# A two-layer graph transformer on one core: where the attention steps stand in the feed-forward loop, and the order of a block's last matmuls

## The chip, the cores and the metric

The kernel runs on one core of a Trainium2 chip. The metric is the device time of one execution in microseconds; the median of three runs is compared.

## The reference

There are 2708 nodes with 512 features each, and an adjacency matrix that is symmetric, sparse and has ones on the diagonal. Two layers of the same form, with weights of their own, follow each other. All is float32.

```python
mask = adj + eye(n)
q, k, v = (h @ W.T + b).reshape(n, 8, 64)            # for Wq, Wk, Wv
scores = einsum('nhd,mhd->hnm', q, k) / sqrt(64)
scores = where(mask == 0, -1e9, scores)
ctx = einsum('hnm,mhd->nhd', softmax(scores), v).reshape(n, 512)
h1 = layer_norm(h + ctx @ Wo.T + bo)
h2 = layer_norm(h1 + relu(h1 @ W1.T + b1) @ W2.T + b2)   # W1: 2048 x 512, W2: 512 x 2048
```

## The kernel before

The first stage turns the adjacency matrix into lists of neighbours. The nodes are sorted by the length of their lists and cut into 22 tiles of up to 128 nodes, so that all the nodes of a tile need about equally many neighbours: from 22 (tile 0) down to 3 (tile 21). The attention of a tile gathers its neighbours' keys and values row by row with indirect DMAs that POOL issues (`gather`, L976), in steps of two neighbours.

Tiles are worked on in pairs, called blocks. Tile 21, the last, has only 20 nodes. There are 11 blocks to a layer, in this order: (21, 20), (19, 18), (8, 9), (7, 10), (6, 11), (0, 17), (1, 16), (2, 15), (3, 14), (4, 13), (5, 12). I number them k = 0 to 10.

The feed-forward part of a block (`feed_forward`) runs over 16 chunks f of 128 hidden units. For each chunk TensorE makes `pf` (the first matrix product, L1290), ScalarE turns it into `ft` with a relu (L1298), and TensorE adds the second product into the accumulators `a0` and `a1` of the block's two tiles (`second`, L1278). The second product runs LAG = 3 chunks behind the first. The last three chunks of it therefore come after the loop, in what I call the tail of the block. `pf` has three buffers in PSUM, `ft` four in SBUF.

The attention of later blocks is written between those chunks. `attend` is a generator, and each turn of it issues one step: VectorE multiplies the gathered keys with the queries (`kv`, L1013) and sums them to scores (`sc`, L1019); one turn later ScalarE takes two exponentials (`p`, L1032) and scales the values by them with eight instructions (`kv` or `acc`, L1039), and VectorE scales the other half (L1045) and adds (L1052). After a tile's last step ScalarE divides with eight instructions (L1083), and the tile's context `cx` is ready. There are three `cx` buffers.

How many turns are taken is set by `advance`. Each call adds credit, at most 1.5 in all; turns are taken while there is credit and fewer than CXB - 1 = 2 contexts wait in `got`. The main loop calls it after each chunk, with PACE (0.62 in the first layer, 0.72 in the second), or with 1.1 or 0.4 in block 0.

In chunk 10 of a block (11 in the very first) `through(k + 1)` takes whatever turns are still missing for the contexts of the next block. Then `attended` turns the two contexts around (TensorE `tp`, L1122; ScalarE `cT`, L1127), and in the next chunk it multiplies them with Wo (`o`, L569) and normalizes the sum (`h`). After chunk 15 `turned` turns `h` around on TensorE, and ScalarE writes it as `hT` in eight copies (L1127). `hT` is the input of the next block's first `pf`. At the beginning of a block VectorE adds `a0` and `a1` to `h` (L1310) and normalizes; in the first layer `keys_values` then makes keys and values for the second layer in chunks 5 to 8.

TensorE, ScalarE and SyncE run in the order in which the program is written. VectorE and POOL run in an order that the framework chooses, except in some stages ahead of the blocks and, for POOL, in block 0 of the first layer. [...]

Of the kernel before, what the change touches and what calls it, by code (L numbers as in the profile page):

```python
# [25 lines left out]
NFC = FF // P  # L26
# [12 lines left out]
LAG = 3  # L39
KVB = 5  # L40
CXB = 3
# [7 lines left out]
PACE = (0.62, 0.72)  # L49
# [422 lines left out]
def by_edges(ctx: ExitStack, tc: tile.TileContext, x, xT, adj, layers, out, good):  # L472
# [57 lines left out]
    def matrix(w, name, tag, by=None):  # L530
        src = chunked(w[name])
        t = wts.tile([P, src.shape[1], src.shape[2]], F32, tag=tag, name=tag)
        if by:
            by.dma_start(out=t, in_=src)
            return t
        k = max(1, src.shape[1] // 4)
        for c in range(0, src.shape[1], k):
            nc.sync.dma_start(out=t[:, c : c + k, :], in_=src[:, c : c + k, :])
        return t
# [32 lines left out]
    def finish(steps):  # L572
        for _ in steps:
            pass
# [6 lines left out]
    def size(g):  # L581
        return min(P, N - g * P)
# [520 lines left out]
    def norm(z, r, gain, shift):  # L1103

        st = small.tile([P, 6], F32, tag="st", name="st")
        nc.vector.bn_stats(st[:r], z[:r])  # L1106
        mv = small.tile([P, 2], F32, tag="mv", name="mv")
        nc.vector.bn_aggr(mv[:r], st[:r])
        va = small.tile([P, 1], F32, tag="va", name="va")
        nc.vector.tensor_scalar(va[:r], mv[:r, 1:2], EPS, None, ALU.add)  # L1110
        rd = small.tile([P, 1], F32, tag="rd", name="rd")
        nc.gpsimd.tensor_tensor(rd[:r], va[:r], mhalf[:r], ALU.pow)  # L1112
        nc.vector.scalar_tensor_tensor(
            z[:r], z[:r], mv[:r, 0:1], gain[:r], ALU.subtract, ALU.mult
        )
        nc.vector.scalar_tensor_tensor(z[:r], z[:r], rd[:r], shift[:r], ALU.mult, ALU.add)  # L1116
# [14 lines left out]
    class Layer:  # L1131
# [133 lines left out]
        def feed_forward(self, block, hs, hT):  # L1265

            w = sum(size(g) for g in block)
            accs = [ps_a.tile([P, DM], F32, tag=f"a{i}", name=f"a{i}") for i in range(len(block))]
            fts = []

            def second(f, only=None):
                c0 = 0
                for g, a in zip(block, accs):
                    r = size(g)
                    if only not in (None, g):
                        c0 += r
                        continue
                    nc.tensor.matmul(  # L1278
                        a[:r],
                        fts[f][:, c0 : c0 + r],  # L1280
                        self.w2[f // 2][:, f % 2, :],
                        start=(f == 0),
                        stop=(f == NFC - 1),
                    )
                    c0 += r

            for f in range(NFC):
                pf = ps_f.tile([P, DM], F32, tag="f", name="pf")
                for c in range(NC):
                    nc.tensor.matmul(  # L1290
                        pf[:, :w],
                        self.w1[f // 2][:, c, f % 2 * P : f % 2 * P + P],
                        hT[:, c, :w],
                        start=(c == 0),
                        stop=(c == NC - 1),
                    )
                ft = dn.tile([P, 2 * P], F32, tag="ft", name="ft", bufs=4)
                nc.scalar.activation(ft[:, :w], pf[:, :w], AF.Relu, bias=self.b1[:, f : f + 1])  # L1298
                fts.append(ft)
                if f >= LAG:  # L1300
                    second(f - LAG)
                yield None
            for g in block:
                for f in range(NFC - LAG, NFC):
                    second(f, g)
            zs = []
            for g, a, h in zip(block, accs, hs):
                r = size(g)
                z = h
                nc.vector.tensor_tensor(z[:r], a[:r], h[:r], ALU.add)  # L1310
                norm(z, r, self.g2, self.e2)
                if self.n == NL - 1:
                    nc.gpsimd.indirect_dma_start(  # L1313
                        out=out,
                        out_offset=bass.IndirectOffsetOnAxis(ap=ident_i[:r, g : g + 1], axis=0),
                        in_=z[:r],
                        in_offset=None,
                        bounds_check=N - 1,
                        oob_is_err=False,
                    )  # L1320
                zs.append(z)
            yield zs
# [41 lines left out]
    blocks = [(NT - 1, NT - 2), (NT - 3, NT - 4)] + [  # L1364
        (i, NT - 5 - i) for i in (*range(8, 5, -1), *range(6))
    ]
    NB = len(blocks)
    order = [g for block in blocks for g in block]
# [47 lines left out]
    credit = 0.0  # L1416

    def advance(more):

        nonlocal credit  # L1420
        credit = min(credit + more, 1.5)
        while credit > 0 and len(got) < CXB - 1:
            cost = next(ahead, None)
            if cost is None:
                break
            credit -= cost

    def through(k):

        while blocks[k][-1] not in got:  # L1430
            next(ahead)

    got = {}
# [38 lines left out]
    for n in range(NL):  # L1472
        last = n == NL - 1
        nxt = None if last else Layer(n + 1, layers[n + 1])
        if n > 0:
            streamed = now.queries(order[8 : 2 * AHEAD])
            got = {}
# [25 lines left out]
        for k, block in enumerate(blocks):  # L1503
            more = k + 1 < NB
            asking = iter(())
            if n > 0 and k + AHEAD < NB:
                asking = now.queries(blocks[k + AHEAD])
            for f, zs in enumerate(now.feed_forward(block, hs, hT)):
                if f == NFC:
                    break  # L1510
                if f in (5, 6, 7, 8) and behind:
                    next(behind)
                if more and f == 10 + (k + n == 0):
                    through(k + 1)
                    projecting = now.attended(blocks[k + 1], got)
                    next(projecting)
                if more and f == 11 + (k + n == 0):
                    for hs_next in projecting:
                        advance(0.5 if k else 0.0)
                advance(PACE[n] if k else 1.1 if f < 11 else 0.4)  # L1520
                if f in (0, 3, 7, 9):
                    next(asking, None)
                if more and f == NFC - 1:
                    finish(asking)
                    hT = now.turned(blocks[k + 1], hs_next)
                if k == 0 and len(now.w1) < NFC // 2 and f % 2 == 0:
                    now.load_w1(len(now.w1), nc.scalar)
                    now.load_w2(len(now.w2), nc.scalar)
                if n > 0 and (k, f) == (0, 2):
                    now.load_second(1, temp)  # L1530
                if not last:
                    if (k, f) == (0, 10):
                        now.load_next()
                        now.kv = [matrix(nxt.w, "Wk", "wk", nc.scalar)]
                    if (k, f) == (0, 13):
                        now.kv.append(matrix(nxt.w, "Wv", "wv", nc.scalar))
                    if (k, f) == (3, 2):
                        now.wq = matrix(nxt.w, "Wq", "wq")
                    if f == 1 and k in (1, 3):
                        i, name, scale = (1, "bk", 1.0) if k == 1 else (0, "bq", DK**-0.5)  # L1540
                        turning = turned_row(now.cols[i], name, scale)
                        rows_of = now if k == 1 else nxt
                        setattr(rows_of, name, next(turning))
                    if f == 3 and k in (1, 3):
                        finish(turning)
                if not last and not more:
                    if f % 2:
                        nxt.load_w1(f // 2)
                        if f > 2:
                            nxt.load_w2(f // 2 - 1)  # L1550
                    if f == 6:
                        nxt.load_first()
                        nxt.load_second(0, temp)
                    if f == 7:
                        finish(ahead)
                        pool += nxt.preloaded(order[:8], temp)
            in_order.close()
            if not last:
                behind = now.keys_values(block, zs)
            if more:  # L1560
                hs = hs_next
# [76 lines left out]
```

## Time and profile before

| what | value |
|---|---|
| median of three runs | 1969.64 us (1968.0 to 1970.87) |
| the profiled execution | 1975.51 us, its span 1973.8 us |
| TensorE busy | 1902.7 us, 96% of the span |
| VectorE busy | 1300.5 us, 66% |
| ScalarE busy | 933.5 us, 47% |
| POOL busy | 794.1 us, 40% |
| mean granted TensorE clock | 0.985 |

The profiled execution took 1.7 us more than its span, and 5.9 us more than the median of the runs. The span has these parts: keys, values and the neighbour lists of the first layer (to 170 us), its queries (to 275 us), its 11 blocks (to 1141 us), a stage of queries again (to 1238 us), and the second layer's blocks. [...] Lost time is better seen where a matmul starts later than the one before it allows. The share of VectorE in the whole span says little, because the last two blocks of each layer have next to no attention left, while others are full of it.

### The profile page before, as it was taken

What the parts mean: (1) busy time and instruction counts of PE and PEld (TensorE: products, weight loads), DVE (VectorE), ACT (ScalarE), POOL (GpSimd) and SP (SyncE); (2) the same over time, 40 slices, a digit from 0 to 9 for tenths busy, and PEclk for the clock granted to TensorE, in tenths of its full rate; (3) what the DMA queues carried; (4) which work ended last, traced back from release to release, by engine and by line L of the source; (5) the groups of instructions that cost most, each with busy time, mean ns of one, the idle gap of its engine ahead of it and who ended that gap; (6) DMA issues with size and microseconds to landing.
All of it is one profiled execution on the core that took longest, in us unless ns stands there. A gap on an engine that the chain in (4) does not pass through costs nothing. (4 is left out here: it accounts for less than half of the span.)

```text
span 1973.8 us, 20851 instructions
## 1 busy us (share of the span) xinstructions
PE 1902.7 (96%) x6150; PEld 1102.7 (56%) x6150; DVE 1300.5 (66%) x2141; ACT 933.5 (47%) x3218; POOL 794.1 (40%) x710
## 2 busy tenths in 40 slices
PE   8999989999999999999999998999999999999997
PEld 4443344565656556566566643556666566666664
DVE  6884577684957869558442026887688988877421
ACT  4560244464555655547442112756456765755310
POOL 3114435453645636435210022555346655544210
PEclk9999999999999999999999999999999999999998
DMA  9998667454645647445310646856455766554100
GB/s 331 348 307 286 216 223 258 160 174 166 223 149 190 215 158 237 156 161 187 132 58 22 224 155 231 284 182 215 153 184 192 250 201 221 181 192 148 39 11 13
DMA packets 131487, 366.92 MB, mean 186 GB/s; under 512 B 16669, under 2 KB 36989, under 8 KB 128655
## 3 DMA queue, kind: packets, MB, share of 16 engines
q0 software_dynamic: 69120, 246.35, 37.8%
q1 hardware_dynamic: 53332, 99.66, 14.8%
q10 hardware_dynamic: 8910, 19.48, 2.6%
q8 instruction: 50, 0.82, 0.2%
q14 instruction: 75, 0.61, 0.1%
HBM read 314.62 MB, written 50.83 MB: 185 GB/s over the span
## 5 line engine op out<-in xcount | busy, mean ns | idle before, releaser
L976 POOL DMA_INDIRECT kv<-kv_d,idx x420 | 545.0, 1298 | 475.7 <-DVE acc L1052 313.5
L1278 PE MATMUL a<-w,ft 128*128 128x512 f32 (+1 forms) x1408 | 665.8, 598 | 11.0 <-ACT ft L1298 9.4
L1290 PE MATMUL pf<-hT,w 128*128 128x256 f32 (+1 forms) x2816 | 639.9, 374 | 14.4 <-ACT ft L1298 9.9
L1290 PEld LDWEIGHTS pf<-hT,w 128*128 128x128 f32 x2816 | 523.4, 192 | 193.5 <-issue 106.9
L1278 PEld LDWEIGHTS a<-w,ft 128*128 128x128 f32 (+1 forms) x1408 | 255.8, 186 | 236.6 <-issue 198.7
L1298 ACT ACTIVATE ft<-pf,b 128x256 f32<-128x256 f32 (+1 forms) x352 | 158.5, 459 | 434.0 <-PE pf L1290 433.6
L1013 DVE TENSOR_TENSOR kv<-kv,q 128x1024 f32<-128x1024 f32 (+3 forms) x222 | 256.4, 1158 | 155.0 <-DMA kv<-kv_d,idx 90.3
L1039 ACT ACTIVATE kv<-kv,p 128x64 f32<-128x64 f32 x1232 | 311.0, 334 | 5.0
L1019 DVE TENSOR_REDUCE sc<-kv 128x16 f32<-128x1024 f32 (+3 forms) x222 | 255.0, 1154 | 1.4
L1052 DVE TENSOR_TENSOR acc<-acc,kv 128x1024 f32<-128x1024 f32 (+2 forms) x178 | 203.9, 1146 | 28.7 <-ACT kv L1039 27.9
L1112 POOL TENSOR_TENSOR rd<-va,mhalf 128x1 f32<-128x1 f32 (+1 forms) x88 | 85.2, 968 | 272.2 <-DVE va L1110 270.5
L1032 ACT ACTIVATE p<-sc,minus 128x8 f32<-128x8 f32 (+1 forms) x420 | 103.3, 295 | 154.3 <-DVE sc L1019 154.0
L1045 DVE TENSOR_TENSOR kv<-kv,p 128x512 f32<-128x512 f32 (+1 forms) x178 | 121.5, 683 | 55.8 <-ACT p L1032 55.8
L569 PE MATMUL o<-wo,cT 128*128 128x512 f32 (+1 forms) x352 | 155.1, 593 | 0.5 <-ACT cT L1127 0.5
L569 PEld LDWEIGHTS o<-wo,cT 128*128 128x128 f32 (+1 forms) x352 | 65.1, 186 | 86.5 <-issue 74.5
L1083 ACT ACTIVATE cx<-acc,su 128x64 f32<-128x64 f32 (+1 forms) x352 | 88.4, 333 | 37.8 <-DVE su L1075 31.3
L1310 DVE TENSOR_TENSOR h<-a,h 128x512 f32<-128x512 f32 (+1 forms) x44 | 29.7, 677 | 106.8 <-PE a L1278 106.7
L1116 DVE SCALAR_TENSOR_TENSOR h<-h,rd,ln_b 128x512 f32<-128x512 f32 (+1 forms) x88 | 65.8, 748 | 50.8 <-POOL rd L1112 50.8
L663 ACT ACTIVATE code<-aj 128x2708 bf16<-128x2708 int32 (+1 forms) x22 | 73.3, 3333 | 48.7 <-POOL aj L659 47.4
L666 DVE MAX8 tops<-code 128x8 f32<-128x247 f32 (+2 forms) x242 | 83.1, 400 | 19.2 <-ACT code L663 19.2
L1349 POOL DMA_INDIRECT kv_d<-kvs,ident_i x22 | 23.7, 1078 | 178.7 <-ACT kvs L1343 112.6
L1039 ACT ACTIVATE acc<-kv,p 128x64 f32<-128x64 f32 (+1 forms) x352 | 88.8, 334 | 1.4
(133 smaller groups left out, 1517.0 us busy)
## 6 DMA issues: line engine op xcount, KB each, us to landing
aj<-in_adj SPq DMA_DIRECT2D x21, 1354.0 KB, 7.6
kv_d<-kvs ACTq DMA_DIRECT2D x21, 512.0 KB, 7.0
w<-in_W SPq DMA_DIRECT2D x20, 512.0 KB, 4.7
xg<-in_xT SPq DMA_DIRECT2D x19, 512.0 KB, 8.2
kv<-kv_d,idx POOLq DMA_INDIRECT x420, 5.6
w<-in_W ACTq DMA_DIRECT2D x12, 512.0 KB, 6.0
q_d<-qs SPq DMA_DIRECT2D x22, 256.0 KB, 3.1
zT_d<-zT SPq DMA_DIRECT2D x22, 256.0 KB, 4.8
```

The source lines that it names most:

```text
L569: nc.tensor.matmul(o[:r], xs(c), wm[:, c, :], start=(c == 0), stop=(c == NC - 1))
L976: nc.gpsimd.indirect_dma_start(out=to, out_offset=None, in_=table[:, :], in_offset=bass.IndirectOffsetOnAxis(ap=s, axis=0), bounds_check=N ...
L1013: nc.vector.tensor_tensor(kv[:r, :c, :DM], kv[:r, :c, :DM], self.q[:r].unsqueeze(1).to_broadcast([r, c, DM]), ALU.mult,)
L1019: nc.vector.tensor_reduce(self.sc[:r, s0 : s0 + c, :], kv[:r, :c, :DM].rearrange("p s (h d) -> p s h d", d=DK), AX.X, ALU.add,)
L1032: nc.scalar.activation(p[:r, s, :], self.sc[:r, s, :], AF.Exp, bias=minus[:r, g, s : s + 1])
L1039: nc.scalar.activation(to[:, i, hd], kv[:r, i, DM + h * DK : DM + (h + 1) * DK], AF.Copy, scale=p[:r, s0 + i, h : h + 1],)
L1045: nc.vector.tensor_tensor(to[:, 0, :].rearrange("p (h d) -> p h d", d=DK), kv[:r, 0, DM:].rearrange("p (h d) -> p h d", d=DK), p[:r, s0, : ...
L1052: nc.vector.tensor_tensor(self.acc[:r, :c, :], self.acc[:r, :c, :], kv[:r, :c, DM:], ALU.add)
L1083: nc.scalar.activation(cx[:r, hd], self.acc[:r, 0, hd], AF.Copy, scale=self.su[:r, h : h + 1])
L1278: nc.tensor.matmul(a[:r], fts[f][:, c0 : c0 + r], self.w2[f // 2][:, f % 2, :], start=(f == 0), stop=(f == NFC - 1),)
L1290: nc.tensor.matmul(pf[:, :w], self.w1[f // 2][:, c, f % 2 * P : f % 2 * P + P], hT[:, c, :w], start=(c == 0), stop=(c == NC - 1),)
L1298: nc.scalar.activation(ft[:, :w], pf[:, :w], AF.Relu, bias=self.b1[:, f : f + 1])
```

## The change

Three edits.

1. In the tail of a block, the last three chunks of the second product are issued chunk by chunk, each for both tiles: 13 for the block's first and second tile, then 14 for both, then 15 for both. Before, all three came for the first tile and then all three for the second. The last block of a layer keeps the old order.
2. A third context may wait in `got`. With two waiting, turns go on only where the newer of the two has an odd place of at least 5 in the order of tiles (counted from 0), which means that it is the second tile of its block, from block 2 on.
3. In block 0 of the first layer no attention is issued after chunk 1.

```diff
@@ feed_forward
-            for g in block:
+            if block == blocks[-1]:
+                for g in block:
+                    for f in range(NFC - LAG, NFC):
+                        second(f, g)
+            else:
                 for f in range(NFC - LAG, NFC):
-                    second(f, g)
+                    second(f)
@@ advance
         credit = min(credit + more, 1.5)
-        while credit > 0 and len(got) < CXB - 1:
+        while credit > 0 and len(got) < CXB:
+            newest = max(map(order.index, got), default=0)
+            if len(got) == CXB - 1 and (newest < 5 or newest % 2 == 0):
+                break
             cost = next(ahead, None)
@@ main loop
-                advance(PACE[n] if k else 1.1 if f < 11 else 0.4)
+                if n or k or f != 1:
+                    advance(PACE[n] if k else 1.1 if f < 11 else 0.4)
```

## The prediction

> **What bounds the kernel now.** I read the page's busy times first, then a table of stretches, one for each block (from a block's first `pf` to the next block's), and then the instructions in order of time around the gaps.
>
> ```profile
> span 1973.8 us, 20851 instructions
> PE 1902.7 (96%) x6150; PEld 1102.7 (56%) x6150; DVE 1300.5 (66%) x2141; ACT 933.5 (47%) x3218; POOL 794.1 (40%) x710
> ```
>
> TensorE is the bound: every block waits for it in the end. The table's columns are the stretch, its length, then PE, PEld, DVE, ACT and POOL busy. The first three lines are blocks 3, 4 and 9 of layer one, the others blocks 2, 3, 4, 5 and 9 of layer two.
>
> ```profile
> 513.06:592.27 79.21, 79.21 (x273) 48.97 (x272) 55.30 (x75) 40.74 (x152) 38.79 (x31) 1.00 0.54 178
> 592.27:679.59 87.32, 81.88 (x266) 49.43 (x264) 69.31 (x91) 49.42 (x189) 50.16 (x38) 0.96 0.62 202
> 999.92:1078.24 78.32, 78.32 (x266) 48.08 (x265) 22.04 (x45) 19.93 (x63) 7.26 (x7) 1.00 0.07 27
> 1372.15:1444.77 72.62, 71.01 (x241) 43.91 (x239) 50.60 (x76) 36.23 (x137) 32.17 (x27) 1.00 0.55 178
> 1444.77:1508.99 64.22, 63.98 (x224) 41.09 (x224) 50.01 (x66) 35.04 (x132) 33.50 (x25) 1.00 0.50 172
> 1508.99:1578.77 69.78, 66.64 (x225) 42.50 (x226) 67.86 (x93) 47.28 (x182) 46.27 (x35) 0.98 0.74 244
> 1578.77:1647.24 68.47, 65.67 (x225) 41.66 (x224) 60.04 (x83) 43.72 (x168) 37.60 (x32) 0.98 0.66 220
> 1841.36:1905.18 63.82, 63.82 (x225) 41.28 (x225) 17.33 (x44) 14.53 (x44) 6.32 (x7) 1.00 0.02 9
> ```
>
> Blocks 9 have no attention beside them, so 78.3 and 63.8 us are the price of TensorE's work alone (block 3's 79.2 has a turned row more). What a block takes above that is all that a better order can win. By the same table layer one's blocks 1, 2, 4, 5, 6, 7 and 8 exceed it by 3.0, 8.2, 9.0, 2.7, 2.6, 0.9 and 0.9 us; layer two's 2 to 8 by 2.0, 0.4, 6.0, 4.7, 0.4, 0.4 and 2.0 (block 2 against block 1, which also projects queries). Together 43 us, and block 0 of layer one comes on top:
>
> ```profile
> 287.50 2.34 PE L1290 MATMUL pf<-hT,w 128*128 128x148 f32 x8 [5.97 <-ACT ft L1298]
> ...
> 304.17 2.12 PE L1290 MATMUL pf<-hT,w 128*128 128x148 f32 x8 [2.70 <-ACT ft L1298]
> ...
> 308.94 1.17 PE L1290 MATMUL pf<-hT,w 128*128 128x148 f32 x8
> ```
>
> Two waits for `ft`, and behind each a `pf` that takes 2.1 to 2.3 us in place of 1.17. ScalarE at that time:
>
> ```profile
> 284.64 0.49 ACT L1032 ACTIVATE p<-sc,minus 128x8 f32<-128x8 f32 x2 [5.29 <-DVE sc L1019]
> ...
> 287.09 0.36 ACT L1298 ACTIVATE ft<-pf,b 128x148 f32<-128x148 f32 x1
> ...
> 289.79 2.00 ACT L1083 ACTIVATE cx<-acc,su 128x64 f32<-128x64 f32 x8
> 291.70 0.36 ACT L1298 ACTIVATE ft<-pf,b 128x148 f32<-128x148 f32 x1
> ```
>
> An exponential waits for VectorE, and `ft` 1 stands behind it. Then ScalarE has no pause until 300 us. The largest later wait is at block 4's turning of the contexts:
>
> ```profile
> 643.95 1.91 PE L1122 MATMUL tp<-ident,cx 128*128 128x128 f32 x4 [3.75 <-ACT cx L1083]
> 645.65 3.62 PE L1290 MATMUL pf<-hT,w 128*128 128x256 f32 x8
> ...
> 657.71 1.89 PE L1290 MATMUL pf<-hT,w 128*128 128x256 f32 x8
> ```
>
> And a tail with attention after chunk 15, the end of block 5:
>
> ```profile
> 757.31 2.02 ACT L1083 ACTIVATE cx<-acc,su 128x64 f32<-128x64 f32 x8
> 759.23 2.14 ACT L1127 ACTIVATE hT<-tp,b 128x128 f32<-128x128 f32 x8
> 760.64 2.66 PE L1290 MATMUL pf<-hT,w 128*128 128x256 f32 x8 [2.27 <-ACT hT L1127]
> ```
>
> [...] block 4 of layer two is busy for 66.6 of 69.8 us and still 6.0 us over. [...] here waits of 2.27 us and more are followed by `pf` at up to twice its time[...], and each avoided long wait saves up to 1.7 us more. [...]
>
> **The change, part by part.** Numbers of instructions stay the same; only places change.
>
> *No attention after chunk 1.* One step and one division move from ahead of `ft` 2 to behind it: 2 exponentials (0.48), 8 scalings (2.0) and 8 divisions (2.0), 4.5 us. `ft` 1 keeps its place, so the 5.97 us stay. `ft` 2 comes at 287.8, `ft` 3 to 5 at 292.6, 295.7 and 298.4, each ahead of TensorE's chunk. Late next is `ft` 6 at 304.1, wanted at 304.3. The second wait goes (2.70), and the slow matmuls behind it (0.95 for `pf`, 0.8 for `a`). **Gain 4.4 us**, between 0 and 4.5. VectorE has the same steps one chunk later, with chunks 6 to 10 free of attention behind them. ScalarE's own weight loads for chunk 10 on keep their order and are issued within 1 us of their present times; I cost them at nothing.
>
> *The tail by chunks.* The first tile's product of chunk 14 is wanted 0.86 us later and that of 15 1.72 us later (a product takes 0.86). But the next block's first `pf` needs five of the eight `hT` copies, which ScalarE takes up only after `ft` 15 and the step behind it. In most tails with a wait they set the end as well: they would have let `pf` start at most 0.1 to 0.3 us earlier. Only block 5 of layer two, whose `ft` 14 was there and 15 not, wins some 1.5 us. **Gain 2 us**, 0 to 4. The price: the first accumulator is finished 1.72 us later. VectorE has its addition early in the next block and may hold attention behind it. Its buffer is wanted again 6.9 us after the tail, so TensorE doesn't wait where VectorE keeps up. In a block that fills VectorE up to 1.7 us are lost; taking four such blocks, **a loss up to 7 us**.
>
> *The third context.* Following `advance` through both kernels gives the neighbour rows in each block. Layer one, blocks 0 to 9: before 19, 23, 20, 21, 27, 22, 22, 20, 19, 1; after 19, 23, 21, 24, 23, 22, 24, 22, 16, 0. Layer two: before 27, 26, 18, 20, 27, 24, 20, 20, 20, 0; after 27, 26, 26, 27, 25, 23, 20, 21, 7, 0. A row costs VectorE some 1.7 us ((55.3 - 22.0) / 20 more rows in layer one).
> - Layer one, block 4: the two contexts are there two chunks before they are turned, and 4 rows fewer lie beside it. Of 9.0 us I expect 8.
> - Blocks 2, 5 and its follower 6: a block's last division comes one or two chunks earlier, so that block 5's no longer stands behind chunk 15; 8.2, 2.7 and 2.6 us become about 5, 0.5 and 1: 7 us.
> - Blocks 7 and 8: 1.5 us.
> - Layer two, block 4: both contexts are there a block earlier (4 of 6.0 us); block 5: no division before `ft` 15 (3.6); blocks 2 and 8: 1 and 2. Together 10.6 us.
> - The loss: block 3 now has 27 rows and its tail a step and a division after chunk 15. VectorE would need 17.3 + 27 x 1.7 = 63 of 64 us. I put it at what block 4 shows without its wait for contexts (about 1.5) and the tail above (2.3 + 1.7): 5.5 us. Block 2, now 26 rows, adds a wait of VectorE's of some 4 us (the mean excess of layer two's blocks 4 and 5 is 5.3).
>
> The gathers on POOL and SP's fetches of queries move with these steps, up to a tile earlier. They cost nothing while POOL waits for VectorE to free a buffer ("POOL kv L976 <- DVE acc L1052", 313.5 us in the list of waits); in a full block the reverse is bounded by VectorE's own wait for gathers, 90.3 us over 32 times, 2.8 us each, none of it taken.
>
> **The sum**: 4.4 + 2 + 8 + 7 + 1.5 + 10.6 - 5.5 - 4 = 24; with the whole 7 us of held additions, 17. I take **17 us**, because waits taken from one place tend to be partly found at another and no run shows the new order. 1975.5 - 17 = 1958.5 for an execution like the profiled one; that one stands 5.9 us above the median of the runs, so 1969.6 - 17 is about **1953 us**.
>
> **The rivals.**
> - *Only the two plain waits go.* Block 0 (4.4) and block 4's contexts (3.75 + 1.7) are won, about 10 us, and of the rest VectorE's queue gives most back, since it has the same 1300 us to do: 7 to 10 us, 1961. For it: ScalarE waits for `sc` 154 us in all, and the steps behind that stay as many. Against: blocks at 20 rows lose under 1 us, and more blocks come near that.
> - *VectorE becomes the bound* in layer two's blocks 1 to 4, which follow each other with 25 to 27 rows. A backlog isn't worked off there, scores come late, `ft` waits behind exponentials. At block 4's present excess, 6 us in each of four blocks and in layer one's two with 24 rows: 36 us, against 28.5 recovered (the gains above without those of layer two's blocks 2 and 4): **+7.5 us, 1977**. It decides from about 95% of VectorE in a block (97% in block 4 now). Against: block 1 has 26 rows today in 70.6 us without a loss.
> - *Nothing measurable*: gains and losses of 10 to 15 us cancel, 1970. That the third context is never used is excluded by the counted rows.
>
> **Chances.** Forecast 0.68, first rival 0.17, VectorE as the bound 0.08, nothing 0.07. Within 0.2% (3.9 us, about what can be told from no change here) lie the last and some of the first rival. The range runs from 33 us of gain (all the gains above without a loss) to the first rival's edge: 1937 to 1967.
>
> **What would show it.** Right: one wait for `ft` in block 0, no wait at the turning of contexts in either block 4, layer one's block 4 under 81 us, layer two's block 3 above 67. Wrong: layer two's blocks 1 to 4 each above their 70.6, 70.6, 63.8 and 63.8 by 5 us, or VectorE idle for `a` at the head of full blocks.

## The result and the profile after

The changed kernel takes **2035.89 us** (median of six runs, 2031.6 to 2037.91), the kernel before 1970.1 us beside it: a ratio of 1.0332, with an interval from 1.0319 to 1.0346. The forecast was 1953 us, 17 less than before. It is 66 more.

The head of the page of the kernel after:

```profile
span 2036.2 us, 20826 instructions
...
PE 1919.3 (94%) x6150; PEld 1107.9 (54%) x6150; DVE 1308.1 (64%) x2141; ACT 933.1 (46%) x3218; POOL 805.6 (40%) x710
```

On each of these engines the number of instructions is that of before (the total above also counts register, branch and semaphore instructions), and VectorE's busy time has grown by 7.6 us only. So there is no more work. The span is 62.4 us longer. TensorE's busy time takes 16.6 of that, at a mean granted clock of 0.974 in place of 0.985. The rest is waiting, and the table of stretches says where. The columns are as before: the stretch, its length, PE, PEld, DVE, ACT, POOL busy, clock, DMA share, GB/s. The lines are blocks 0, 3 and 4 of layer one, then 1 to 5 of layer two:

```profile
274.44:357.29 82.85, 64.04 (x224) 31.67 (x225) 54.52 (x75) 38.49 (x152) 37.97 (x33) 0.88 0.65 220
529.64:616.04 86.40, 81.76 (x272) 49.48 (x273) 64.91 (x85) 43.87 (x164) 48.88 (x35) 0.98 0.59 191
616.04:704.30 88.26, 81.63 (x265) 48.91 (x264) 60.98 (x84) 44.86 (x169) 39.69 (x34) 0.96 0.51 167
1337.82:1410.91 73.09, 70.80 (x242) 44.20 (x240) 59.63 (x82) 46.14 (x178) 35.77 (x28) 1.00 0.55 184
1410.91:1494.27 83.36, 75.36 (x241) 46.06 (x240) 65.28 (x91) 46.17 (x178) 44.11 (x34) 0.94 0.63 208
1494.27:1574.10 79.83, 68.54 (x225) 42.58 (x223) 68.10 (x89) 46.27 (x179) 44.20 (x35) 0.94 0.62 203
1574.10:1640.92 66.82, 64.47 (x224) 40.99 (x224) 59.96 (x81) 44.14 (x170) 36.58 (x30) 1.00 0.64 210
1640.92:1713.02 72.10, 67.15 (x225) 42.74 (x225) 60.64 (x82) 42.13 (x162) 41.36 (x30) 0.95 0.60 201
```

Block 0 went from 69.2 to 82.9 us, block 3 of layer one from 79.2 to 86.4, layer two's blocks 2 and 3 from 72.6 and 64.2 to 83.4 and 79.8. VectorE is busy for 65.3 of 83.4 us in block 2 and for 68.1 of 79.8 in block 3: in both it also stands idle for a good part. (Its 68.1 us in block 3 are more than the 63.8 us that TensorE's work alone takes, so some 4 us of that block's loss, by my estimate from these two numbers, would be there without any idling.) What VectorE waits for is in the list of waits (engine and line waited for, us in total, times, longest). After:

```profile
DVE kv L1013 <- DMA kv<-kv_d,idx: 222.6, 83, 9.2
...
PE tp L1122 <- DVE h L1116: 27.8, 10, 6.5
...
PE pf L1290 <- ACT ft L1298: 22.7, 4, 10.5
...
PE v L569 <- DVE kvs L1345: 14.5, 6, 5.5
...
PE a L1278 <- DVE h L1314: 11.6, 6, 5.1
```

and what corresponds in the kernel before, where the third stood at 9.9 us, and the fifth at 1.6 us under another name (`PE a L1278 <- DVE va L1110`):

```profile
DVE kv L1013 <- DMA kv<-kv_d,idx: 90.3, 32, 13.7
...
PE v L569 <- DVE kvs L1341: 4.3, 2, 2.3
...
PE tp L1122 <- DVE h L1116: 0.8, 1, 0.8
```

VectorE's products with gathered keys wait 132 us longer for their gathers, at 83 places in place of 32. VectorE is busy for 64% of the span, so that this alone needn't cost time; but four waits of TensorE grow with it: for the normalized `h` of the next block, for `ft` (10.5 us at once in block 0), for VectorE's copies of the second layer's keys (`kvs`; the longest, 5.5 us, is in layer one's block 4), and for the addition that frees an accumulator. (L1314 and L1345 are L1310 and L1341 of before; edit 1 moved them by four lines.) The experiments take these apart, except for the third.

### The profile page after: what moved, and what is told of

It is laid out like the page before. It is cut to its first block, busy times and chain, and to the rows that moved or that the text cites. A ratio compares the mean times of both kernels' runs of the same rounds, so it can differ in the third digit from the quotient of the medians.

```text
span 2036.2 us, 20826 instructions
## 1 busy us (share of the span) xinstructions
PE 1919.3 (94%) x6150; PEld 1107.9 (54%) x6150; DVE 1308.1 (64%) x2141; ACT 933.1 (46%) x3218; POOL 805.6 (40%) x710
## 5 line engine op out<-in xcount | busy, mean ns | idle before, releaser
L1278 PE MATMUL a<-w,ft 128*128 128x512 f32 (+1 forms) x1408 | 677.5, 607 | 12.1 <-DVE h L1314 11.6
L1013 DVE TENSOR_TENSOR kv<-kv,q 128x1024 f32<-128x1024 f32 (+3 forms) x222 | 256.8, 1160 | 233.3 <-DMA kv<-kv_d,idx 222.6
L1278 PEld LDWEIGHTS a<-w,ft 128*128 128x128 f32 (+1 forms) x1408 | 259.4, 190 | 245.7 <-issue 208.0
L1052 DVE TENSOR_TENSOR acc<-acc,kv 128x1024 f32<-128x1024 f32 (+2 forms) x178 | 204.0, 1146 | 18.6 <-ACT kv L1039 16.5
L1314 DVE TENSOR_TENSOR h<-a,h 128x512 f32<-128x512 f32 (+1 forms) x44 | 29.1, 679 | 132.8 <-PE a L1278 132.8
L569 PE MATMUL v<-wv,zT 128*128 128x512 f32 (+1 forms) x176 | 86.7, 639 | 14.5 <-DVE kvs L1345 14.5
L666 DVE MAX8 tops<-code 128x8 f32<-128x247 f32 (+2 forms) x242 | 83.2, 402 | 20.5 <-ACT code L663 20.3
L1347 ACT COPY kvs<-v 128x512 f32<-128x512 f32 (+1 forms) x22 | 12.9, 586 | 176.6 <-PE v L569 105.0
L1116 DVE SCALAR_TENSOR_TENSOR h<-h,rd,ln_b 128x512 f32<-128x512 f32 (+1 forms) x88 | 65.8, 748 | 42.8 <-POOL rd L1112 42.7
```

What stands on the lines that cost most here:

```text
L569: nc.tensor.matmul(o[:r], xs(c), wm[:, c, :], start=(c == 0), stop=(c == NC - 1))
L1013: nc.vector.tensor_tensor(kv[:r, :c, :DM], kv[:r, :c, :DM], self.q[:r].unsqueeze(1).to_broadcast([r, c, DM]), ALU.mult,)
L1052: nc.vector.tensor_tensor(self.acc[:r, :c, :], self.acc[:r, :c, :], kv[:r, :c, DM:], ALU.add)
L1278: nc.tensor.matmul(a[:r], fts[f][:, c0 : c0 + r], self.w2[f // 2][:, f % 2, :], start=(f == 0), stop=(f == NFC - 1),)
```

## The experiments

Every ratio is to the kernel before, in runs on the same chip. Block lengths in the table are from a block's first `pf` to the next block's, in us, worked out from each kernel's trace in the same way. "Pause" is the run e4 below.

| block | before | after | edit 3 | edit 2 | edits 1, 2 | edit 2, pause | edit 2, pause in 8 and 9 | edit 2, norms first |
|---|---|---|---|---|---|---|---|---|
| layer one, 0 | 69.2 | 82.9 | 79.5 | 70.0 | 72.0 | 71.5 | 70.2 | 69.0 |
| 3 | 79.2 | 86.4 | 79.2 | 87.5 | 87.0 | 79.2 | 83.2 | 81.7 |
| 4 | 87.3 | 88.3 | 87.1 | 85.7 | 89.1 | 87.3 | 80.6 | 82.4 |
| 5 | 81.1 | 83.5 | 81.1 | 86.1 | 85.0 | 80.8 | 80.9 | 87.0 |
| 6 | 80.9 | 88.1 | 80.9 | 84.1 | 89.2 | 80.9 | 80.1 | 85.3 |
| layer two, 1 | 70.6 | 73.1 | 70.6 | 76.7 | 76.8 | 70.6 | 70.6 | 78.0 |
| 2 | 72.6 | 83.4 | 72.6 | 87.5 | 82.5 | 70.6 | 82.4 | 77.1 |
| 3 | 64.2 | 79.8 | 64.2 | 75.6 | 79.1 | 63.7 | 64.4 | 69.3 |
| 4 | 69.8 | 66.8 | 68.8 | 70.4 | 66.6 | 64.7 | 69.6 | 70.2 |
| 5 | 68.5 | 72.1 | 68.5 | 63.7 | 70.8 | 65.8 | 63.7 | 70.2 |

### The three edits alone, and two together

Edit 3 alone:

```diff
-                advance(PACE[n] if k else 1.1 if f < 11 else 0.4)
+                if n or k or f != 1:
+                    advance(PACE[n] if k else 1.1 if f < 11 else 0.4)
```

> The kernel before with edit 3 alone (no attention after chunk 1 of the first block). Theory A (each edit costs where it changes VectorE's order): in this block alone VectorE's order differs from before, a multiplication that waits for its gather now stands ahead of the addition that frees the next gather's buffer. The whole cost that the changed kernel shows in block 0 of layer one (82.9 against 69.2 us, 13.7) comes from here: 13 us slower than before, with a wait of some 10 us for ft in block 0. Theory B (the third context alone fills VectorE and delays everything): no cost here, or the gain of 4.4 us of the prediction.

Measured: 1982.14 us against 1969.64, 1.0056 (1.0036 to 1.0076). All of it is in block 0, with 10.9 us of waiting for `ft` at one place.

Edit 1 alone (the tail chunk by chunk, the last block of a layer as before):

> The kernel before with edit 1 alone (the tail by chunks). Theory A: VectorE takes both additions of a1 and a0 together at the head of each block, the first norm and with it POOL's power (rd) come later, gathers queue behind it on POOL, and blocks 1 to 8 of both layers lose some us each: 15 to 30 us slower. Theory B: within 3 us of before, since products of TensorE are only exchanged and nothing waits for the first tile's sum.

Measured: 1974.97 us, 1.0022 (1.0011 to 1.0033). That is some 4 us, between the two expectations. Its profile shows no block worse by more than 2 us, and so not where they lie; the two tails that gain, layer one's 6 and layer two's 5, win 1.7 and 1.5 us.

Edit 2 alone (the third context in `advance`):

> The kernel before with edit 2 alone (a third context may wait). Theory A: 20 to 35 us slower, most of it in blocks 2 and 3 of layer two (26 and 27 rows of neighbours each), where the changed kernel loses 10.8 and 15.6 us more than the kernel before. Theory B: all of the 66 us. Theory C (the prediction): 10 to 20 us faster, and the tail's order is what spoils it.

Measured: 2009.41 us, 1.019 (1.0148 to 1.0233). This is the main loss, 37 us by the ratio and 40 by the medians, of the 66.

Edits 1 and 2 together:

> Edits 1 and 2 together, without edit 3. The three edits alone come to 11 + 4.4 + 37 us = 52, all together to 65. If the missing 13 us are edits 1 and 2 disturbing each other, this gives 2020 to 2027, with layer one's block 6 and layer two's blocks 3 and 5 each 4 us or more above the third context alone. If they are edit 3 with edit 2 (block 0 took 82.9 us there and 79.5 alone, and block 1 got 5 us longer), it gives 2009 to 2016.

Measured: 2023.42 us, 1.0269 (1.0247 to 1.0291), where the two by themselves multiply to 1.0212. So edits 1 and 2 disturb each other by some 11 us, as far as edit 2's wide interval tells. Edit 3 adds its 0.6% on top (1.0332 / 1.0269). Two waits of TensorE grow by more than the two edits have of them separately. One is at the head of blocks. The timeline of TensorE with edits 1 and 2 (start, us, engine, line, operation, in brackets the idle time before it and what ended it), at the heads of layer two's blocks 2 and 5:

```profile
1408.55 2.66 PE L1278 MATMUL a<-w,ft 128*128 128x512 f32 x4 [2.42 <-DVE h L1314]
...
1636.14 1.98 PE L1278 MATMUL a<-w,ft 128*128 128x512 f32 x4 [1.64 <-DVE h L1314]
```

The new block's accumulator waits until VectorE has added the old one away. By edit 1 the first accumulator is finished 1.72 us later (two products of 0.86 us), and by edit 2 VectorE has more in front of the addition. In some versions the releaser at this place is a step of the norm (`va`) in place of the addition; with both names counted, TensorE waits 1.6 us in the kernel before, 4.7 with edit 2 alone, 2.4 with edit 1 alone, 8.8 with the two, 11.6 with all three. The other wait is for `kvs`: 4.3 us before, 5.7 with edit 2, 4.8 with edit 1, 10.8 with the two, 14.5 with all three. Together these account for some 8 of the 11 us (3.3 and 4.6, what the two edits have beyond the sum of their own increases). Why layer two's block 5 takes 7.1 us longer with the two than with edit 2 alone, and block 2 5.0 less, stays open.

### Where edit 2 loses: norms behind a product that waits

TensorE turns `h` around at the end of a block. With edit 2 alone it finds `h` not ready 12 times, for 40.1 us in all, above all in layer one's blocks 3 to 6 and layer two's 1 to 3. The timeline of TensorE with edit 2 alone, at the end of layer two's block 1:

```profile
1382.19 0.60 PE L1122 MATMUL tp<-ident,h 128*128 128x128 f32 x4
1386.33 1.11 PE L1122 MATMUL tp<-ident,h 128*128 128x128 f32 x4 [3.54 <-DVE h L1116]
```

VectorE ahead of it: the addition `acc`, the product, the two additions of `o` with which the norms begin, and the second norm's last step:

```profile
1359.95 1.23 DVE L1052 TENSOR_TENSOR acc<-acc,kv 128x1024 f32<-128x1024 f32 x1
1366.56 1.23 DVE L1013 TENSOR_TENSOR kv<-kv,q 128x1024 f32<-128x1024 f32 x1 [5.38 <-DMA kv<-kv_d,idx]
...
1374.90 0.68 DVE L1248 TENSOR_TENSOR h<-o,xb 128x512 f32<-128x512 f32 x1
...
1379.36 0.68 DVE L1248 TENSOR_TENSOR h<-o,xb 128x512 f32<-128x512 f32 x1
...
1385.54 0.74 DVE L1116 SCALAR_TENSOR_TENSOR h<-h,rd,ln_b 128x512 f32<-128x512 f32 x1
```

The same instructions in the kernel before, in the same block with the same 26 rows beside it:

```profile
1350.02 0.68 DVE L1248 TENSOR_TENSOR h<-o,xb 128x512 f32<-128x512 f32 x1
...
1353.04 0.66 DVE L1248 TENSOR_TENSOR h<-o,xb 128x512 f32<-128x512 f32 x1
...
1359.46 0.75 DVE L1116 SCALAR_TENSOR_TENSOR h<-h,rd,ln_b 128x512 f32<-128x512 f32 x1 [0.46 <-POOL rd L1112]
```

In before, the first tile's `o` is finished at 1349.1 and its norm begins at 1350.0; the second norm ends at 1360.2, and TensorE turns `h` at 1366.1: 6 us to spare. With edit 2 the first tile's `o` is finished at 1364.1, and its norm begins only at 1374.9. Until 1366.6 VectorE stands 5.4 us in front of a product whose keys haven't landed; then it takes 8 us of attention steps that also stand ahead of the norm. The norms need no gather, but stand behind all this. The second is finished 7.1 us before the next block's `pf` at 1393.4, where in before it was 11.9.

That an instruction of VectorE stands behind one that waits, though its own input is there, is seen in the trace of a run further down, with a pause in chunks 8 and 9: a norm's step of 0.15 us whose input is there at 1414.9 us is taken at 1421.4, behind a product that VectorE waits 5.29 us to begin.

Whether this is what costs was tested by moving the steps. With a pause: in chunks 6 to 11 the old limit of two holds, so that no attention is written just ahead of the norms.

```diff
-    def advance(more):
+    def advance(more, three=True):
...
-            if len(got) == CXB - 1 and (newest < 5 or newest % 2 == 0):
+            if len(got) == CXB - 1 and (newest < 5 or newest % 2 == 0 or not three):
...
-                        advance(0.5 if k else 0.0)
-                advance(PACE[n] if k else 1.1 if f < 11 else 0.4)
+                        advance(0.5 if k else 0.0, False)
+                advance(PACE[n] if k else 1.1 if f < 11 else 0.4, not 6 <= f <= 11)
```

> Edit 2 alone, but with the old limit of two waiting contexts in chunks 6 to 11 of a block. Layer one then has its old order; layer two has 27, 26, 22, 22, 23, 24, 22, 22, 14 rows in blocks 0 to 8. Theory Q (steps that are written in chunks 6 to 11 stand ahead of the norms of the next block in VectorE's queue, and their gathers haven't landed): the loss of 37 us is gone, and block 4 of layer two keeps the gain of the earlier contexts: 2 to 8 us faster than before. Theory V (more rows in a block fill VectorE): blocks 2 to 4 of layer two still lose 5 us or more: 5 to 15 us slower than before.

Measured: 1957.59 us against 1967.62, 0.9937 (0.9912 to 0.9961): 10 us faster, a little more than theory Q had. The wait for `h` is down to 3.2 us, and layer two's blocks 2 to 4 are at the price of TensorE's work or near it:

```profile
1371.22:1441.80 70.58, 70.58 (x242) 44.14 (x241) 58.04 (x84) 39.07 (x149) 36.88 (x31) 1.00 0.66 217
1441.80:1505.51 63.71, 63.71 (x226) 41.17 (x226) 55.37 (x74) 40.14 (x153) 40.06 (x28) 1.00 0.61 199
1505.51:1570.21 64.70, 63.87 (x225) 40.98 (x223) 59.03 (x83) 42.81 (x165) 37.61 (x30) 1.00 0.65 217
```

This version differs in its rows too, though (22 in blocks 2 and 3, where edit 2 has 26 and 27). So a second one, with the pause in chunks 8 and 9 alone (`not 8 <= f <= 9` in the main loop), keeps the rows:

> The third context as in the change, but in chunks 8 and 9 of a block the old limit of two holds. By the counted turns the blocks keep the neighbour rows of the third context alone within two each (layer one 19, 23, 21, 24, 23, 22, 22, 24, 16, 0; layer two 27, 26, 26, 25, 25, 25, 20, 21, 7, 0). What changes is VectorE's order: in layer one's blocks 3 and 6 and layer two's blocks 1 and 2 no product with gathered keys stands ahead of the first norm's end or between the two; in layer one's blocks 4 and 7 and layer two's block 3 one still does. Theory (products that wait for gathers, ahead of the next block's norms, make the loss): layer one's block 3 back at 79 to 81 us (87.5 with the third context alone), layer two's block 1 at 70.6 to 71.5 (76.7), block 2 at 70.5 to 73 (87.5), block 3 at 66 to 71 (75.6); some 1967 us in all, 1959 to 1976. Rival (it is the amount of attention beside a block that costs, wherever VectorE has it): rows are the same, so at least two thirds of the 37 us stay, 1992 or more, and layer two's blocks 2 and 3 stay above 78 and 70.

Measured: 1972.51 us against 1970.76, 1.0002 (0.9989 to 1.0014). With the rows of edit 2 within two in every block, the loss in the whole is gone, so the amount of attention beside a block can't be what makes most of it. Block by block my expectation was half right. Layer two's blocks 1 and 3 are at 70.6 and 64.4, and layer one's block 4 at 80.6, the lowest of all versions; layer one's block 3, at 83.2, is above the 79 to 81 expected. But block 2 of layer two stayed at 82.4, as the rival had it. Edit 2 alone made layer two's blocks 1 to 4 longer by 33.0 us together; of these 9.8 are left, all in block 2, and gains in other blocks make up for them. I had put the product that holds the norms into block 3. The timeline of VectorE shows it at the end of block 2, inside the first norm, between its aggregate and its next step (the profile names no releaser for this wait):

```profile
1414.76 0.17 DVE L1108 BATCH_NORM_AGGREGATE mv<-st 128x2 f32<-128x6 f32 x1
1420.21 1.22 DVE L1013 TENSOR_TENSOR kv<-kv,q 128x1024 f32<-128x1024 f32 x1 [5.29 <-issue]
1421.36 0.15 DVE L1110 TENSOR_SCALAR va<-mv 128x1 f32<-128x1 f32 x1
```

TensorE waits only 1.24 us for `h` there. Its larger waits in this block are for `ft`, behind an exponential that waits 10.88 us for VectorE:

```profile
1430.04 0.49 ACT L1032 ACTIVATE p<-sc,minus 128x8 f32<-128x8 f32 x2 [10.88 <-DVE sc L1019]
```

```profile
1433.00 1.13 PE L1278 MATMUL a<-w,ft 128*128 128x512 f32 x2 [2.54 <-ACT ft L1298]
1438.57 6.51 PE L1278 MATMUL a<-w,ft 128*128 128x512 f32 x8 [4.45 <-ACT ft L1298]
```

The product at 1420.21 was late, and VectorE summed it to a score only at 1428.80, after both norms. So one late product delays the norms, and the norms in turn delay the scores behind them. In layer one's block 4 a product stands inside the norms as well, but waits only 1.3 us (at 657.14), and TensorE only 1.7. So it isn't the order by itself: in these two blocks a product inside a norm costs more where VectorE waits longer for it.

The opposite test holds the products back by force: with edit 2, each product written from chunk 11 on goes behind the last norm written before it on VectorE.

```diff
+            for end in normed * freed:
+                tc.add_manual_dep(product.ins, end.ins.name, ...)  # order only, no wait
```

> Edit 2 alone, with the same steps in the same chunks, but VectorE must take the two norms of the next block ahead of every product with the queries that is written from chunk 11 on; the orders of TensorE and ScalarE stay those of edit 2 alone. Theory Q: the norms are ready when TensorE turns them around, blocks 3 to 6 of layer one and 1 to 4 of layer two come back to within some 3 us of the kernel before: from 8 us faster to 10 us slower than before, against 37 slower with edit 2 alone. What may be late instead is the exponentials that ScalarE has ahead of ft. Theory V: the rows are the same and so is the loss, 30 us or more.

Measured: 2019.23 us, 1.0244 (1.0213 to 1.0274). The total is what theory V expected, and slower than edit 2 alone; the trace shows other waits. The wait for `h` is gone (1.8 us left), and layer two's blocks 2 and 3 fell from 87.5 and 75.6 to 77.1 and 69.3. But layer two's blocks 3 to 7 now all take 69.3 to 70.2 us, 5.5 to 6.4 above the price of TensorE's work, also 6 and 7, which paid nothing before, and in layer one blocks 1 and 5 to 8 are 4 to 7 us longer than before. The scores come later, and ScalarE, whose order is as written, waits for them with `ft` behind: TensorE waits 59.8 us for `ft` (`pf` and `a` together), 13.9 with edit 2 alone. ScalarE's longest item in the list of waits, 154.0 us in before and 108.3 with edit 2 alone, is now

```profile
ACT p L1043 <- DVE sc L1030: 274.1, 65, 13.9
```

I read this as a window between `o` and the turning of `h` that is too short for both in a full block; no run shows that by itself. The forced order takes away the wait for `h` and puts one for `ft` in its place, so it doesn't decide between the theories. The runs with a pause do, for most of the loss: with fewer steps there, it goes.

A last rival for layer two was the lead of the gathers, three steps ahead of their products (EARLY). The kernel before with two:

```diff
-EARLY = 3
+EARLY = 2
```

> The kernel before, with gathers issued two steps ahead of their use in place of three. VectorE's order in layer two stays. Theory Q (what VectorE waits for is the landing of gathers, and their lead is what the pause in chunks 6 to 9 gives): the gathers of the steps in chunks 10 and 11 are nearer to their use; VectorE waits for gathers more than the 90 us of before, and the kernel is 5 to 25 us slower. Rival (gathers are limited by when buffers come free, and five buffers set that whatever the lead): within 3 us.

Measured: 1977.85 us, 1.0049 (1.0034 to 1.0065). In size this is theory Q's: 10 us slower, and VectorE waits 135.9 us for gathers in place of 90.3. But the loss lies in blocks 0 and 4 of layer one, 5 us each, and no block of layer two is longer than before. A shorter lead costs, but doesn't bring about edit 2's pattern.

### Block 0: an addition behind a product

In block 0 the forecast of ScalarE's order was right, `ft` 2 came early, and the wait of 2.70 us is gone; a longer one took its place. TensorE after, with the first wait that was there before:

```profile
286.80 2.34 PE L1290 MATMUL pf<-hT,w 128*128 128x148 f32 x8 [6.02 <-ACT ft L1298]
...
315.17 2.34 PE L1290 MATMUL pf<-hT,w 128*128 128x148 f32 x8 [10.45 <-ACT ft L1298]
```

ScalarE has a division ahead of that `ft`, and the division waits for VectorE:

```profile
312.83 2.02 ACT L1083 ACTIVATE cx<-acc,su 128x64 f32<-128x64 f32 x8 [8.76 <-DVE su L1075]
```

VectorE and POOL after:

```profile
298.01 1.23 DVE L1013 TENSOR_TENSOR kv<-kv,q 128x1024 f32<-128x1024 f32 x1 [5.46 <-DMA kv<-kv_d,idx]
299.15 1.22 DVE L1052 TENSOR_TENSOR acc<-acc,kv 128x1024 f32<-128x1024 f32 x1
...
307.76 1.23 DVE L1013 TENSOR_TENSOR kv<-kv,q 128x1024 f32<-128x1024 f32 x1 [5.54 <-DMA kv<-kv_d,idx]
308.90 1.22 DVE L1052 TENSOR_TENSOR acc<-acc,kv 128x1024 f32<-128x1024 f32 x1
```

```profile
289.13 0.99 POOL L976 DMA_INDIRECT kv<-kv_d,idx  x1 [0.30 <-issue]
300.64 0.99 POOL L976 DMA_INDIRECT kv<-kv_d,idx  x1 [10.52 <-DVE acc L1052]
301.94 1.14 POOL L976 DMA_INDIRECT kv<-kv_d,idx  x1 [0.30 <-issue]
310.39 1.20 POOL L976 DMA_INDIRECT kv<-kv_d,idx  x1 [7.31 <-DVE acc L1052]
```

This is a lockstep. The product waits for its gather; the addition behind it on VectorE frees the buffer of the next gather; POOL can issue that one only then, and the next product waits for it. In each of the two turns shown VectorE waits about as long as a gather takes to land: 5.46 and 5.54 us, where the median over the whole kernel is 5.7. In the kernel before the addition stood ahead of the product, and POOL ran on:

```profile
293.17 1.22 DVE L1052 TENSOR_TENSOR acc<-acc,kv 128x1024 f32<-128x1024 f32 x1
295.50 1.23 DVE L1013 TENSOR_TENSOR kv<-kv,q 128x1024 f32<-128x1024 f32 x1 [1.11 <-DMA kv<-kv_d,idx]
```

Two suspects: this order, or the weight loads (two of 512 KB) which ScalarE now issues at the same time as the gathers. First the loads, moved behind chunk 3:

```diff
-                if k == 0 and len(now.w1) < NFC // 2 and f % 2 == 0:
+                if k == 0 and len(now.w1) < NFC // 2 and f in ((0, 3, 4) if n == 0 else (0, 2, 4)):
```

> Edit 3 alone, with the second pair of weight loads of block 0 issued after chunk 3 in place of chunk 2. With edit 3 alone they were issued at 288.6 us, with the gathers of 286.7 and 289.1; in the kernel before at 292.6. VectorE's order in block 0 is then a third one. Theory L (the loads delay the gathers on the DMA engines): block 0 of layer one comes back from 79.5 to 66 to 71 us. Theory O (VectorE's order, with a product that waits for its gather ahead of the addition that frees a buffer): it stays above 75 us if that order persists.

Measured: 1968.7 us, 1.0003 (0.999 to 1.0016), block 0 at 72.2. This didn't separate the two, as the framework changed its order again with the edit (a product at 287.01 us still stands ahead of its addition at 288.15, the next one doesn't). So the order alone, with the loads left where edit 3 has them; in chunks 3 to 5 of block 0 a product goes behind the last addition written before it:

```diff
+            for end in added[-1:] * ordered:      # ordered: block 0, 3 <= f <= 5
+                tc.add_manual_dep(product.ins, end.ins.name, ...)  # order only, no wait
```

> Edit 3 alone with its weight loads where the edit has them, and with VectorE's order mended: a product with gathered keys written in chunks 3 to 5 of block 0 of layer one goes behind the last addition (acc, L1052) written before it. If the order makes the loss (the addition that frees the next gather's buffer stands behind a product that waits for a gather), POOL's waits of 10.3 us for acc go, block 0 falls from 79.5 us to 68 to 72, and the whole to 1966 to 1972. If the weight loads issued beside the gathers make it, the product of about 296 us still comes 8 to 9 us after its gather's issue, the long wait for ft stays at 8 us or more, and the whole stays at 1977 to 1983.

Measured: 1968.94 us against 1970.76, 0.9987 (0.9977 to 0.9997); block 0 falls from 79.5 to 69.1. POOL in that stretch (its waits for `acc` now carry line 1064):

```profile
286.95 0.99 POOL L976 DMA_INDIRECT kv<-kv_d,idx  x1 [0.30 <-issue]
289.40 1.20 POOL L976 DMA_INDIRECT kv<-kv_d,idx  x1 [1.46 <-DVE acc L1064]
290.90 1.26 POOL L976 DMA_INDIRECT kv<-kv_d,idx  x1 [0.30 <-issue]
294.02 1.73 POOL L976 DMA_INDIRECT kv<-kv_d,idx  x1 [1.86 <-DVE acc L1064]
```

The order was it: the loads are where edit 3 has them, and the loss is gone. But the 4.4 us of the forecast don't appear either: of 2.70 us of waiting 1.26 remain ahead of `pf` at 304.89, and 1.50 us of a wait for `h` at 336.03 are new. 1.8 us of the median is what edit 3 is worth with its order mended, and the profiles don't show where: block 0 takes 69.1 us, in before 69.2.

### What is left of the change

Edit 1 on top of the pause:

> The third context with the pause in chunks 6 to 11 (1957.6 us in its own runs), and edit 1. By itself edit 1 made 4.4 us more of the median, with gains of 1.6 us each in layer one's block 6 and layer two's block 5. If what it costs comes from VectorE's new order at the heads of full blocks only where norms are late, nothing is lost here: 1954 to 1961. If both additions at once, ahead of the attention that waits there, cost in any order, 1961 to 1968.

Measured: 1968.7 us against 1970.76, 0.9989 (0.9977 to 1.0001). The pause alone had 0.9937, so edit 1 takes back about 0.5%, some 10 us, the side of the second expectation and a little beyond it. What it costs at the head of a block is small. The longest such wait of TensorE is this one; with the pause alone it waits 1.80 us at the same place (for `va`), so that edit 1 adds 0.8:

```profile
436.17 1.98 PE L1278 MATMUL a<-w,ft 128*128 128x512 f32 x4 [2.63 <-DVE h L1314]
```

By blocks the loss is spread: 2.8 us in layer two's block 4, 1.9 in layer one's 1, 1.6 in layer two's 5, the others about 1 or less. I haven't found one cause for all of it.

The pause, with edit 3 in its mended order and without edit 1:

> The third context with the pause in chunks 6 to 11, and edit 3 with VectorE's order mended; edit 1 left out. Edit 3 so mended gave 1.8 us of the median by itself, in block 0 of layer one; the third context with the pause gave 10, in layer two's blocks 2 to 5. They lie in different places, so they should add: 0.6% under the kernel before, 0.3 to 0.8%, some 1958 us where the kernel before stands at 1970. Rival: the gain of the pause was partly that session's, or the two meet in blocks 1 and 2; then within 0.3% of before.

Measured: **1956.41 us against 1966.33, 0.9943 (0.9922 to 0.9964)**. It beats both kernels, and can't be told from the pause alone.

## Why the prediction was wrong

**The step that failed** is a sentence in the part on edit 3, "VectorE has the same steps one chunk later". The parts on edits 2 and 1 shared it without saying so: the steps were counted as if VectorE kept its order between them. The orders of ScalarE and TensorE can be read off the program. VectorE's is chosen by the framework, it is a result of the change, and it is where the time went. In block 0 it made a wait of 10.5 us for `ft`; at the ends of full blocks it held up the norms, and TensorE waited 27.8 us for `h` in place of 0.8. The description of the kernel says that VectorE's order is the framework's; the sum didn't use it.

**The term that was put at nothing** is VectorE's wait for gathers, 90.3 us with "none of it taken". It went to 222.6 us. It was read as a bound on the gathers' cost in a full block at 2.8 us a time; but VectorE passed the wait on to what stood behind it (5.29 us of it to a norm's step, in the trace of the pause in chunks 8 and 9), and the price depended on what that was.

Point by point:
- *Edit 3*: 4.4 us gained was the forecast, 0 to 4.5 its bounds; alone it cost 11 us (0.56%). Its ScalarE half came true for `ft` 2 to 5, with VectorE late in place of ScalarE after that. ScalarE's second pair of weight loads, which was to keep its time within 1 us, came 4 us earlier (288.6 against 292.6); the run with the mended order has it early too (287.0).
- *Edit 1*: 2 us gained, or up to 7 us lost by held additions. Alone it lost 0.2%; with edit 2 TensorE's wait for held additions is seen (11.6 us in the whole change, against 1.6 before). With edits 1 and 2 alone it is 8.8 us. Here the mechanism was named, and was stopped too early by "TensorE doesn't wait where VectorE keeps up".
- *Edit 2, layer one*: 16.5 us were to be gained in blocks 2 and 4 to 8. After, those six and block 3 together take 17.9 us longer, and block 1, for which nothing was forecast, 4.4. One term was sound: with the norms in time block 4 takes 80.6 us (pause in chunks 8 and 9), 6.7 under before, where 8 was forecast.
- *Edit 2, layer two*: block 4 gained 3.0 us (4 forecast) and block 8 gained 1.8 (2 forecast), but block 5 lost 3.6 us in place of gaining as much. The losses were sized at 5.5 us in block 3 and 4 in block 2; they are 15.6 and 10.7. The rows were counted right. Their price was too low: the sum has 63 us of VectorE for the 27 rows of block 3, where the prediction's own line for block 4 before shows 67.9 us for as many; after, block 3 has 68.1. Beyond the estimated 4 us that this costs, both losses come with VectorE waiting, not with VectorE full.
- *Of the signs to look for*: the contexts are in time in both blocks 4, as forecast. Block 0 has two waits for `ft`, not one. Layer one's block 4 isn't under 81: TensorE waits there 5.46 us for `kvs` and 1.14 for `h`. Layer two's block 3 is above 67, for more reasons than the one given; blocks 2 and 3 are over the mark that was to show the forecast wrong, 1 and 4 are not. The other mark, VectorE idle for `a` at the head of full blocks, hardly shows (1.3 us at the head of layer two's block 1): it is TensorE that waits there, for VectorE.
- *The rival "VectorE becomes the bound"* named layer two's blocks 1 to 4 and the right sign, and was given 0.08. By the busy times its mechanism explains some 4 us in block 3 and no more: it was to decide from 95% of VectorE (the prediction's own estimate, beside 97% in block 4 of before), and VectorE is busy for 78% of block 2 (65.3 of 83.4) and 85% of block 3 (68.1 of 79.8). Its price, 7.5 us, was a fifth of edit 2's loss.

No version tried has the gain of 17 us. The best one wins 10.

## What to carry to other kernels

Where a framework orders an engine, a change that moves steps in the program can change that engine's order too; compare the orders instruction by instruction before a gain is counted. VectorE held up a norm's step here for the 5.29 us that a product ahead of it waited; so on such an engine look for every instruction that waits for a transfer, and ask what stands behind it: a norm that TensorE needs soon, or the instruction that frees the buffer of the next transfer. Here, work that waits for gathers was best not written just ahead of a dependent chain with a deadline, however idle the engine looked.

## What was not expected of the hardware

**Gathers beside large loads.** Over the whole kernel a gather lands 5.6 us after its issue (median of 420, before). Between 284 and 300 us, with ScalarE's loads of 512 KB issued among them, the median is 5.8 us in before, where the two pairs of loads are issued 7 us apart and took 5.7 us, but 7.7 us in the run with the mended order, where they are issued 4 us apart and the median that the trace gives for ScalarE's loads of this stretch is 11.2 us. In that run more gathers were issued in the stretch as well, 8 in place of 5, so that the loads aren't shown to be the reason, and no run here took it apart further. If they slow the gathers, they may have made the lockstep in block 0 dearer. They weren't its cause: the mended order has the second pair at 287.0 us, where edit 3 alone has it at 287.2, and block 0 falls from 79.5 to 69.1 us.

**Two-sided windows.** Neither order of the two kinds of VectorE work in a block's last chunks was free: with products first TensorE waited 40 us for `h`; with norms first ScalarE waited 166 us more for scores (274.1 against 108.3), and TensorE 46 us more for `ft`. Before these runs I would have taken the forced order for the remedy.
